# Keeping the first batch's y on the chip across a layer boundary, and making attention's first input in a written order

## The chip, the cores and the metric

The kernel runs on one core of a Trainium2 chip. The metric is device time in microseconds for one execution, lower is better. The core has five engines with queues of their own that run in order and wait for each other by semaphores: TensorE (PE, matmuls and transposes, with its weight loads shown apart as PEld), VectorE (DVE), ScalarE (ACT), GpSimd (POOL), and SyncE (SP), which here only issues DMAs. A view called the timeline lists the instructions with their start and length; "us from the span's start" is meant wherever a time of day is given.

## The reference

Input x has 8 batches of 2048 nodes with 256 features; adj is a 2048 by 2048 matrix. Everything is float32. Two layers follow each other:

```
# layer 0: graph convolution with batch norms, then residual and layer norm
A_norm = adj + eye
deg    = colsum(A_norm) + rowsum(A_norm) - diag(A_norm);  dinv = rsqrt(deg)
agg[b] = (A_norm * dinv[:, None] * dinv[None, :]) @ x[b]
h      = relu(batchnorm(agg @ W1.T + b1, g1, be1))      # 512 wide, statistics over all b and n
y      = batchnorm(h @ W2.T + b2, g2, be2)              # 256 wide, statistics over all b and n
x1     = layernorm(x + y)
# layer 1: attention with 4 heads of 64, masked where adj == 0, then residual and layer norm
q, k, v = x1 @ W
out    = layernorm(x1 + softmax(q k^T / 8 + mask) v)
```

The second batch norm needs the statistics of y over all batches before any y can be used. So layer 1 can't begin before layer 0 has ended for every batch.

## The kernel before

**Loading.** 16 row tiles of adj are loaded, turned by TensorE (L228) and copied into quarters T of 128 x 8 x 512 (`t0` to `t7`, 16 KB in a partition each). Row and column sums give dinv: `rsum` (L257, L260 on DVE), then a power on GpSimd (L97, in four pieces). `first_t1` (L208) is two DVE operations that compare and subtract in a quarter. The scheduler orders DVE here; SP and POOL go in the order of the text.

**Layer 0's products.** The aggregation is done with a scheme of seven products for every 2 by 2 block of halves (`product`, L320, eight steps of two matmul instructions), for units `(k, b, d)`: two halves of columns, pairs of batches, two halves of features. A unit needs forms of x: `scale` multiplies by dinv (on ACT for the first unit, L299; on GpSimd later, L293), and `s1` to `s4` (L304 to L318) add and subtract scaled forms on GpSimd. From the quarters, `t2`, `t3`, `t4` (L329 to L339) make differences on DVE. In the first unit the products come in the order p1, p2, p3 (which wants s4), p6 (s2 and t2), p7 (s3 and t3), p4 (t4), p5. `spread_dinv` sends dinv through DRAM into `dbc`, a row copied to all partitions, by which GpSimd scales the results `ag` (L402 and others). `linear` (L349) applies W1 and writes h to DRAM (`h_d`), 1 MB for each chunk of 512 nodes of one batch.

**Layer 0's second linear.** The 32 chunks go in 16 pairs. The first two pairs are made in place from the last unit (L568); the others are read back (`read_h`, L467, SP's queue, seven pairs deep, into slots of the quarters). For each pair ACT applies batch norm and relu (L497), GpSimd makes four forms (L516), PE does seven products (L521), DVE adds them up into `Y` (tiles `ag00` to `ag11`, used in turn by every second pair) and takes statistics (L535). Each Y is written to `y_d` in DRAM (L551, L561). The order of the pairs ends with batch 0: chunks 0 and 1 in the last but one, 2 and 3 in the last. Then `bn2.root` (an aggregate on DVE, L109, and a power on GpSimd) and `bn2.affine` (three small DVE operations, L114 to L116) give the scale `sc2` and shift `sh2`. In all of layer 0 every engine's order is that of the text.

**Attention's input.** `Layer1Input` makes, for a chunk c of a batch: `load_y` (L662) and `load_x` (L666) from DRAM; `bn` (ACT, L670, two instructions); `norm`, a half at a time (PE transposes, L681; a DVE add to x, L685; statistics, L635 and L637); `root` (four small GpSimd operations, L95 to L643); `apply` (ACT, L647, four instructions); `turn` (PE transposes, L703, and an ACT copy into `x1t`, L709); `project` for q (copied by ACT, L740), k (copied by DVE, L742) and v (PE L747, copied by ACT, L754). For batch 0 chunks 0 to 3 are made one after the other ahead of attention, in an order that the scheduler chooses:

```
for c in range(NCH):
    inp.load_y(0, c)
    inp.load_x(0, c)
...
    inp.root(0, c)
    for half in range(2):
        inp.apply(0, c, half)
    for half in range(2):
        inp.turn(0, c, half)
    for w in range(3 if c < NCH - 1 else 0):
        inp.project(0, 0, c, w)
```

`yt`, the place for y, has one buffer.

**Attention.** 64 units (batch, pair of heads, chunk of 512 queries) of 16 steps, one for each tile of 128 keys. A step g has `scores` (PE, L790), `mask_scores` (DVE, L802), `exps` (ACT, L808), `weigh` (PE, L820) and `add_up` (GpSimd, sums of probabilities, L829 and L831). Scores run three steps ahead (`LEAD`). PE, DVE, ACT and POOL follow the text's order here. Other work, the ends of units and the input of later batches, is put into the steps by `at_step(unit, step, ...)`; so are the last chunk's projections of batch 0's first pair of heads, at steps 0.1, 6.1 and 10.1 of unit 0.

The tiles live in pools on one stack: the pools of layer 0 are closed before those of attention open, and new tiles wait for what lay under them.

Of the kernel before, what the change touches and what calls it, by code (L numbers as in the profile page):

```python
# [26 lines left out]
def tile_gcn_then_masked_attention(  # L27
# [15 lines left out]
    nc = tc.nc  # L43
# [91 lines left out]
    with tc.tile_pool(name="bt", bufs=1) as bp, tc.tile_pool(name="x", bufs=1) as xp:  # L135

        def quarter(slot, pool=None):
            return (pool or bp).tile([P, HT, CH], F32, name=f"t{slot}")

        w1s = bp.tile([P, ND, H], F32, name="w1s")  # L140
        st1 = bp.tile([P, NH, NALL, 6], F32, name="st1")
        dinv = bp.tile([P, NT], F32, name="dinv")
        mdiag = bp.tile([P, NT, P], U8, name="mdiag")
        T = {}
        for s, ij in enumerate(HALVES):
            T[0, ij] = quarter(s)
        for s, ij in enumerate(HALVES[:3]):
            T[1, ij] = quarter(4 + s)


        free = [f"x{i}" for i in range(9)]

        class Form:
            def __init__(self):
                self.name = free.pop(0)
                self.t = xp.tile([P, HT, P], F32, name=self.name)

            def done(self):
                free.append(self.name)

        def load_form(b, j, d):
            f = Form()
            nc.sync.dma_start(
                f.t,
                x[b, j * HT * P : (j + 1) * HT * P, d * P : (d + 1) * P].rearrange(
                    "(t p) d -> p t d", p=P
                ),
            )
            return f

        def mask_out(k, ij, m8):
            i, j = ij
            c0 = (j * NK + k) * CH
            nc.sync.dma_start(mask_d[:, i * HT : (i + 1) * HT, c0 : c0 + CH], m8)

        def mask_of(k, ij):

            i, j = ij
            m8 = bp.tile([P, HT, CH], U8, name="m8")
            nc.vector.tensor_scalar(m8, T[k, ij], 0.0, None, op0=ALU.is_equal)  # L180
            if i == j:
                for q in range(TPC):
                    m = k * TPC + q
                    nc.vector.tensor_copy(
                        m8[:, m, q * P : (q + 1) * P], mdiag[:, i * HT + m, :]
                    )
            mask_out(k, ij, m8)

        units = [(k, b, d) for k in range(NK) for b in range(0, B, 2) for d in range(ND)]
        S = {}  # L190

        with tc.tile_pool(name="bt7", bufs=1) as bp7, tc.tile_pool(
            name="stage", bufs=2
        ) as sp, tc.tile_pool(name="stage1", bufs=1) as sp1, tc.tile_pool(
            name="pst", bufs=4, space=PSUM
        ) as pst, tc.tile_pool(name="psc", bufs=1, space=PSUM) as psc, tc.manual_schedule(
            engines={ENG.SP, ENG.Pool}
        ):
            T[1, HALVES[3]] = quarter(7, bp7)
            m8 = bp.tile([P, HT, CH], U8, name="m8")  # L200
            rsum = sp1.tile([P, NT], F32, name="rsum")
            diag = sp1.tile([P, NT], F32, name="diag")

            pc = psc.tile([P, CH], F32, name="pc")
            order = [j * HT + (NK - 1) * TPC + q for j in range(2) for q in range(TPC)]
            order += [j * HT + q for q in range(TPC) for j in range(2)]

            def first_t1(engine, here):  # L208
# [4 lines left out]
            for n, t in enumerate(order):  # L213
# [31 lines left out]
                if k == 0 and j == 1 and q < 2:  # L245
                    first_t1(nc.gpsimd, here)
# [874 lines left out]
```

## Time and profile before

| | |
|---|---|
| median of 3 runs | 3677.39 us (3677.05 to 3677.88) |
| profiled execution | 3676.57 us, of which the profile's span covers 3674.7 us |
| busy: PE | 3595.0 us (98%) |
| busy: POOL / DVE / ACT | 2777.7 (76%) / 1989.6 (54%) / 1642.2 us (45%) |
| granted TensorE clock, mean | 0.989 |

The profile is one execution by the hardware's own profiler. Busy time says how long an engine worked; its idle time is put down to what ended it. Where an engine waited for several others, the last to come is named. A granted clock of 1.00 is TensorE's full clock. The three-run median is 0.8 us above the profiled execution.

### The profile page before, as it was taken

What the parts mean: (1) busy time and instruction counts of PE and PEld (TensorE: products, weight loads), DVE (VectorE), ACT (ScalarE), POOL (GpSimd) and SP (SyncE); (2) the same over time, 40 slices, a digit from 0 to 9 for tenths busy, and PEclk for the clock granted to TensorE, in tenths of its full rate; (3) what the DMA queues carried; (4) which work ended last, traced back from release to release, by engine and by line L of the source; (5) the groups of instructions that cost most, each with busy time, mean ns of one, the idle gap of its engine ahead of it and who ended that gap; (6) DMA issues with size and microseconds to landing.
All of it is one profiled execution on the core that took longest, in us unless ns stands there. A gap on an engine that the chain in (4) does not pass through costs nothing.

```text
span 3674.7 us, 55830 instructions
## 1 busy us (share of the span) xinstructions
PE 3595.0 (98%) x23055; PEld 1490.0 (41%) x23055; DVE 1989.6 (54%) x2927; ACT 1642.2 (45%) x2034; POOL 2777.7 (76%) x1460
## 2 busy tenths in 40 slices
PE   7999999999999889999999999999999999999997
PEld 4444444444444333343433343433343344343332
DVE  6112131221146546766676676676676676667665
ACT  5001101110135345565565565565566566566555
POOL 5434263434247549999999999999999999999996
PEclk9999999999999889999999999999999999999999
DMA  9122232221246400010010010001001001000000
GB/s 330 54 86 77 83 126 92 75 91 35 75 181 254 175 18 1 18 41 13 13 36 24 13 36 24 7 30 36 7 24 36 7 24 35 13 13 30 7 1 25
DMA packets 133465, 207.92 MB, mean 57 GB/s; under 512 B 6976, under 2 KB 114000, under 8 KB 122704
## 3 DMA queue, kind: packets, MB, share of 16 engines
q1 hardware_dynamic: 132880, 199.00, 15.7%
q8 instruction: 183, 3.00, 0.3%
q0 software_dynamic: 144, 4.19, 0.3%
q10 hardware_dynamic: 176, 1.06, 0.1%
q14 instruction: 82, 0.67, 0.1%
HBM read 128.72 MB, written 75.51 MB: 56 GB/s over the span
## 4 chain that ended last, share of the span: by engine, by line
PE 95%; DVE 1%; POOL 1%; DMA 1%; ACT 1%; issue 0%; SPq 0%; DVEq 0%; POOLq 0%; ACTq 0%
PE out_ps L820 25%; PE st L790 24%; PE pa L323 21%; PE pm L735 6%; PE ph L356 5%; PE pa L521 5%; PE pm L747 3%; PE pm L847 2%; PE pm L681 1%; PE pm L703 1%; PE pm L874 1%; PE ps L228 1%; PE pm L861 1%; POOL acc L831 1%; PE ph L568 1%; DMA bt_d<-t 0%
## 5 line engine op out<-in xcount | busy, mean ns | idle before, releaser
L831 POOL TENSOR_TENSOR acc<-acc,prob 128x1024 f32<-128x1024 f32 x823 | 1947.8, 2367 | 103.0 <-ACT prob L808 45.2
L802 DVE SCALAR_TENSOR_TENSOR prob<-mask,st 128x1024 f32<-128x1024 uint8 x1024 | 1243.2, 1219 | 607.5 <-PE st L790 583.5
L808 ACT ACTIVATE prob<-prob 128x1024 f32<-128x1024 f32 x1024 | 1082.4, 1057 | 940.2 <-DVE prob L802 920.4
L820 PE MATMUL out_ps<-prob,v 64*64 64x512 f32 x8192 | 1077.4, 596 | 1.7 <-DVE ot L836 1.7
L790 PE MATMUL st<-qt,kt 64*64 64x512 f32 x8192 | 1066.9, 590 | 1.0 <-DVE prob L802 0.9
L323 PE MATMUL pa<-t,x 128*128 128x512 f32 x1792 | 774.6, 594 | 12.9 <-POOL x L318 9.1
L790 PEld LDWEIGHTS st<-qt,kt 64*64 64x64 f32 x8192 | 313.0, 133 | 568.3 <-issue 530.4
L323 PEld LDWEIGHTS pa<-t,x 128*128 128x128 f32 x1792 | 341.7, 191 | 443.7 <-issue 427.9
L820 PEld LDWEIGHTS out_ps<-prob,v 64*64 64x64 f32 x8192 | 285.6, 133 | 513.4 <-issue 414.3
L402 POOL TENSOR_TENSOR ag<-ag,dbc 128x512 f32<-128x512 f32 x16 | 20.2, 1264 | 459.9 <-DVE ag L401 457.3
L360 ACT ACTIVATE h<-ph,b1s 128x512 f32<-128x512 f32 x112 | 76.9, 687 | 404.4 <-PE ph L356 404.4
L735 PE MATMUL pm<-x1t,wq 128*128 128x512 f32 x512 | 250.8, 614 | 2.4 <-ACT x1t L709 2.4
L384 ACT COPY ag<-pa 128x512 f32<-128x512 f32 x16 | 9.4, 586 | 434.5 <-PE pa L323 434.5
L356 PE MATMUL ph<-ag,w1s 128*128 128x512 f32 x448 | 193.4, 592 | 0.0
L829 POOL TENSOR_TENSOR acc<-prob 128x1024 f32<-128x1024 f32 x64 | 151.0, 2360 | 17.5 <-ACT prob L808 15.9
L647 ACT ACTIVATE x<-x,ln_nm,ln_rs 128x256 f32<-128x256 f32 x256 | 137.5, 586 | 24.3 <-POOL ln_nm L643 24.3
L747 PEld LDWEIGHTS pm<-wq,x1t 128*128 128x128 f32 x1024 | 119.5, 192 | 28.2 <-issue 28.2
L361 DVE BATCH_NORM_STATS2 st<-h 128x6 f32<-128x512 f32 x112 | 76.9, 692 | 99.1 <-ACT h L360 99.1
L735 PEld LDWEIGHTS pm<-x1t,wq 128*128 128x128 f32 x512 | 89.8, 195 | 98.1 <-issue 87.2
L356 PEld LDWEIGHTS ph<-ag,w1s 128*128 128x128 f32 x448 | 85.1, 190 | 107.1 <-issue 106.9
L747 PE MATMUL pm<-wq,x1t 128*128 128x128 f32 x1024 | 128.1, 278 | 0.0
L381 DVE TENSOR_TENSOR ag<-pa,ag 128x512 f32<-128x512 f32 x16 | 11.1, 692 | 203.1 <-PE pa L323 203.1
(126 smaller groups left out, 2553.1 us busy)
## 6 DMA issues: line engine op xcount, KB each, us to landing
x<-in_x_dram SPq DMA_DIRECT2D x96, 512.0 KB, 4.2
h_d<-h SPq DMA_DIRECT2D x28, 1024.0 KB, 3.9
t<-h_d SPq DMA_DIRECT2D x28, 1024.0 KB, 7.0
a<-in_adj_dram SPq DMA_DIRECT2D x16, 1024.0 KB, 5.0
y_d<-ag SPq DMA_DIRECT2D x32, 512.0 KB, 2.9
yt<-y_d SPq DMA_DIRECT2D x32, 512.0 KB, 3.2
out_dram<-x SPq DMA_DIRECT2D x32, 512.0 KB, 2.9
bt_d<-t SPq DMA_DIRECT2D x4, 2048.0 KB, 16.2
```

The source lines that it names most:

```text
L323: nc.tensor.matmul(pa, s.t[:, m, :], t[:, m, :], start=(m == 0), stop=(m == HT - 1))
L356: nc.tensor.matmul(ph, w1s[:, d, f * P : (f + 1) * P], ag[:, d, :], start=(d == 0), stop=(d == ND - 1),)
L521: nc.tensor.matmul(py, w[:, f, :], t[:, f, :], start=(f == 0), stop=(f == 1))
L647: nc.scalar.activation(self.t[:, i, :], self.t[:, i, :], AF.Identity, bias=self.nm[:, i : i + 1], scale=self.rs[:, i : i + 1],)
L735: nc.tensor.matmul(pm, wq[:, d, wcols], xt[:, d, cols], start=(d == 0), stop=(d == ND - 1))
L747: nc.tensor.matmul(pm[:, j * P : (j + 1) * P], xt[:, d, t * P : (t + 1) * P], wq[:, d, wcols], start=(d == 0), stop=(d == ND - 1),)
L790: nc.tensor.matmul(st[r * HD : (r + 1) * HD, h, :], kt[hs, j * P + r * HD : j * P + (r + 1) * HD], qt[hs, cols], start=True, stop=True,)
L802: nc.vector.scalar_tensor_tensor(p, mask[:, j, cols][:, None, :].to_broadcast([P, 2, CH]), MASKED, st, op0=ALU.mult, op1=ALU.add,)
L808: nc.scalar.activation(probs[g], probs[g], AF.Exp)
L820: nc.tensor.matmul(outs[u][hs, r, :], inp.qkv[b, hp][2][rs, j, hs], probs[g][rs, h, :], start=(j == 0), stop=(j == NT - 1),)
L829: nc.gpsimd.tensor_add(accs[u], probs[g - 1], probs[g])
L831: nc.gpsimd.tensor_add(accs[u], accs[u], probs[g])
```

## The change

- The two chunks of Y of each of the last two pairs, batch 0's four chunks, stay in their tiles (`y0`); attention's first input reads them there. They are still written to DRAM.
- Batch 0's x in node order is read into the tiles `h1` and `dbc` (`x0`), by four DMAs on SP's queue ahead of w2 and of the reads of h.
- Pools lie on two stacks, left and right. Layer 0's quarters and forms are on the left and are followed there by the mask, W and attention's input (`attn_in`); the pool `l0` with Y, h and dbc is on the right and is followed there by attention's other tiles. The slots of the quarters that the pairs use are dealt in another order.
- Both `bn2.root` and both `bn2.affine` follow each other after the last pair. W (`wq`) is read on GpSimd's queue, ahead of the mask.
- Batch 0's input is made in the text's order: for all four chunks bn, transposes of y (into the PSUM tiles of the scores), add, statistics and root; then chunk 0's apply, turn, k, q and v; chunk 1's apply and turn; the first three scores, with chunk 1's k and chunk 2's apply behind the second. The rest is put into unit 0 by `at_step`, and chunk 2's and 3's q into units 1 and 2.
- At the start, DVE follows the text's order too, with the add into `rsum` ahead of `first_t1`; in the first unit of products s1 to s4 are on DVE, s3 between t2 and t3; `spread_dinv`'s copy is on ACT.

The diff, without lines that only changed their indentation:

```diff
-    with tc.tile_pool(name="bt", bufs=1) as bp, tc.tile_pool(name="x", bufs=1) as xp:
+    left, right = ExitStack(), ExitStack()
+    bp = left.enter_context(tc.tile_pool(name="bt", bufs=1, side="left"))
+    xp = left.enter_context(tc.tile_pool(name="x", bufs=1, side="left"))
-        with tc.tile_pool(name="bt7", bufs=1) as bp7, tc.tile_pool(
-            name="stage", bufs=2
-        ) as sp, tc.tile_pool(name="stage1", bufs=1) as sp1, tc.tile_pool(
+    with tc.tile_pool(name="bt7", bufs=1, side="right") as bp7, tc.tile_pool(
+        name="stage", bufs=2, side="right"
+    ) as sp, tc.tile_pool(name="stage1", bufs=1, side="right") as sp1, tc.tile_pool(
-            engines={ENG.SP, ENG.Pool}
+        engines={ENG.SP, ENG.Pool, ENG.DVE}
-        with tc.tile_pool(name="l0", bufs=1, reuse_waits="tile") as lp, tc.tile_pool(
+    lp = right.enter_context(
+        tc.tile_pool(name="l0", bufs=1, side="right", reuse_waits="tile")
+    )
+    with tc.tile_pool(
-                nc.vector.tensor_copy(dt, pd)
+            nc.scalar.copy(dt, pd)
-            def s1(v):
+        def s1(v, engine=nc.gpsimd):
-                nc.gpsimd.tensor_add(S[v, 1].t, S[v, 1, 0].t, S[v, 1, 1].t)
+            engine.tensor_add(S[v, 1].t, S[v, 1, 0].t, S[v, 1, 1].t)
...
-            def s4(v):
+        def s4(v, engine=nc.gpsimd):
...
-            for s in (s1, s2, s4, s3):
-                s(0)
+        for s in (s1, s2, s4):
+            s(0, nc.vector)
-                    for t, slot in ((t2, 4), (t3, 5), (t4, 6)):
-                        t(0, slot)
+                t2(0, 4)
+                s3(0, nc.vector)
+                t3(0, 5)
+                t4(0, 6)
-            places = {0: 0, 1: 5}
+        places = {0: 4, 1: 2}
+        x0 = []
+        for n, (name, size) in enumerate((("h1", [P, NH, CH]), ("dbc", [P, N]))):
+            t = lp.tile(size, F32, name=name)
+            t = t if n else t.rearrange("p a b -> p (a b)")
+            for i in range(2):
+                tx = t[:, i * N // 2 : (i + 1) * N // 2].rearrange("p (t d) -> p t d", d=D)
+                nc.sync.dma_start(
+                    tx, x[0, len(x0) * CH : (len(x0) + 1) * CH].rearrange("(t p) d -> p t d", p=P)
+                )
+                x0.append(tx)
-            for n, slot in enumerate((6, 1, 3, 4, 2)):
+        for n, slot in enumerate((0, 5, 6, 1, 3)):
-                if n == len(pairs) - 1:
-                    bn2.root(1)
-            bn2.root(0)
-            bn2.affine(1)
-            bn2.affine(0)
-    mpool = ctx.enter_context(tc.tile_pool(name="mask", bufs=1, reuse_waits="tile"))
+    y0 = [t for n in (len(pairs) - 2, len(pairs) - 1) for t in Y[n]]
+    left.close()
+    mpool = ctx.enter_context(tc.tile_pool(name="mask", bufs=1, side="left", reuse_waits="tile"))
-    nc.sync.dma_start(wq, wqkv.rearrange("(c p) f -> p c f", p=P))
+    with tc.manual_schedule(engines={ENG.DVE, ENG.Pool}):
+        nc.gpsimd.dma_start(wq, wqkv.rearrange("(c p) f -> p c f", p=P))
+        for o in (1, 0):
+            bn2.root(o)
+        for o in (1, 0):
+            bn2.affine(o)
-            self.st = pool.tile([P, n, 6], F32, name="ln_st")
...
+            self.st = pool.tile([P, n, 6], F32, name="ln_st", bufs=NCH)
...
+            self.y_pool = pool
-            y = self.yt[b, c] = self.pool.tile([P, NO, CH], F32, name="yt", bufs=1)
+            y = self.yt[b, c] = self.y_pool.tile([P, NO, CH], F32, name="yt", bufs=1)
-            y = self.yt[b, c]
-            tiles = range(IT * half, IT * (half + 1))
-            for i in tiles:
+            self.turn_y(b, c, half, pm)
+            self.add_y(b, c, half, pm, self.x1[b, c])
+        def turn_y(self, b, c, half, pm):
+            y = self.yt[b, c]
+            for i in range(IT):
+                r0 = (IT * half + i) * P
-                        pm[:, i % IT, o * P : (o + 1) * P], y[:, o, i * P : (i + 1) * P], ident
+                        pm[:, i, o * P : (o + 1) * P], y[:, o, r0 : r0 + P], ident
+        def add_y(self, b, c, half, pm, xt):
+            tiles = range(IT * half, IT * (half + 1))
+            here = slice(tiles[0], tiles[-1] + 1)
-            nc.vector.tensor_add(t[:, tiles[0] : tiles[-1] + 1], pm, t[:, tiles[0] : tiles[-1] + 1])
+            nc.vector.tensor_add(t[:, here], pm, xt[:, here])
-        def project(self, b, hp, c, which):
+        def project(self, b, hp, c, which, k_on_act=False):
+                elif k_on_act:
+                    nc.scalar.copy(dst, pm)
-            name="attn", bufs=2, reuse_waits="tile"
-        ) as ap_, tc.tile_pool(
-            name="ps_s", bufs=2, space=PSUM
-        ) as ps_s, tc.tile_pool(name="ps_o", bufs=1, space=PSUM) as ps_o, tc.tile_pool(
-            name="ps_m", bufs=2, space=PSUM
+            name="attn_in", bufs=2, side="left", reuse_waits="tile"
+        ) as ip, ExitStack() as late, tc.tile_pool(
+            name="ps_s", bufs=2, space=PSUM, reuse_waits="tile"
+        ) as ps_s, tc.tile_pool(
+            name="ps_o", bufs=1, space=PSUM, reuse_waits="tile"
+        ) as ps_o, tc.tile_pool(
+            name="ps_m", bufs=2, space=PSUM, reuse_waits="tile"
-            inp = Layer1Input(ap_, ps_m, NCH + 3)
+            inp = Layer1Input(ip, ps_m, NCH + 3)
+                if b:
+            for j, c in ((0.1, 2), (4.1, 3)):
+                for half in range(2):
+                    at_step(0, j, inp.turn, 0, c, half)
+            for half in range(2):
+                at_step(0, 1, inp.apply, 0, 3, half)
+            for j, c, w in (
+                (1.1, 1, 2), (2.1, 2, 1), (5.1, 2, 2), (6.1, 3, 1), (8.1, 1, 0), (10.1, 3, 2)
+            ):
+                at_step(0, j, inp.project, 0, 0, c, w)
+            for c in (2, 3):
+                at_step(c - 1, 3.1, inp.project, 0, 0, c, 0)
+            with tc.manual_schedule(engines=IN_ORDER):
-                inp.load_y(0, c)
-                inp.load_x(0, c)
+                    inp.yt[0, c] = y0[c]
+                    inp.x1[0, c] = ip.tile([P, TPC, D], F32, name="x1", bufs=NCH + 3)
+                    pm = ps_s.tile([P, TPC, D], F32, name="st")
-                    inp.norm(0, c, half)
+                        pmh = pm[:, half * IT : (half + 1) * IT, :]
+                        inp.turn_y(0, c, half, pmh)
+                        inp.add_y(0, c, half, pmh, x0[c])
+                right.close()
+                ap_ = inp.y_pool = late.enter_context(
+                    tc.tile_pool(name="attn", bufs=2, side="right", reuse_waits="tile")
+                )
+                def ready(c):
+                    if c < 2:
-                for w in range(3 if c < NCH - 1 else 0):
-                    inp.project(0, 0, c, w)
-            with tc.manual_schedule(engines=IN_ORDER):
+                ready(0)
+                inp.project(0, 0, 0, 1, k_on_act=True)
+                inp.project(0, 0, 0, 0)
+                inp.project(0, 0, 0, 2)
+                ready(1)
+                    if g == 1:
+                        inp.project(0, 0, 1, 1)
+                        ready(2)
```

The reads of y for batch 0 and its `load_x` are gone; for the other seven batches nothing is changed in what attention does, step by step.

## The prediction

> **What bounds the kernel now.** I read the page's first two parts, the list of who waited for whom on TensorE, the timeline, and a table of stretches, in that order. The page has TensorE busy for 3595.0 of 3674.7 us, so only about 80 us can come from filling it; a little more lies in matmuls that run at a lowered clock. The waits say where. Columns: who waited for what, us in total, times, longest.
>
> ```profile
> PE pm L703 <- ACT x L647: 16.5, 4, 5.0
> PE pm L681 <- ACT yt L670: 11.1, 1, 11.1
> PE pa L323 <- POOL x L318: 9.1, 1, 9.1
> PE pm L735 <- ACT x1t L709: 2.4, 3, 0.9
> ```
>
> Three of the four lie between the layers, the third at the start of layer 0. The stretches (length, busy us and count of PE, weight loads, DVE, ACT, POOL; then granted clock, DMA share, GB/s) show that the clock adds to this:
>
> ```profile
> 1271.70:1289.50 17.80, 11.85 (x40) 7.00 (x41) 3.69 (x11) 5.84 (x10) 1.68 (x4) 0.59 0.61 200
> 1303.00:1318.20 15.20, 9.09 (x44) 5.72 (x41) 4.96 (x12) 7.44 (x13) 8.71 (x7) 0.84 0.10 34
> 1318.20:1339.50 21.30, 15.39 (x44) 7.83 (x44) 3.74 (x11) 5.08 (x9) 1.66 (x4) 0.66 0.08 25
> 1410.00:3600.00 2190.00, 2188.78 (x18648) 863.19 (x18640) 1488.70 (x2196) 1297.58 (x1542) 2079.53 (x1068) 1.00 0.06 20
> ```
>
> The last line is attention at work: PE idle 1.2 us of 2190 at full clock, so whatever is won before it reaches the end. The first three are its entrance, idle and at a clock of 0.59 to 0.84.
>
> **Part 1, the start of layer 0.** The timeline there (start, length):
>
> ```profile
> 62.65 9.45 ACT L299 ACTIVATE x<-x,dinv 128x128 f32<-128x128 f32 x32 [4.07 <-POOL dinv L97]
> 69.84 5.74 POOL L306 TENSOR_TENSOR x<-x,x 128x1024 f32<-128x1024 f32 x1 [4.29 <-ACT x L299]
> 82.15 6.40 POOL L318 TENSOR_TENSOR x<-x,x 128x1024 f32<-128x1024 f32 x1
> 88.60 41.64 PE L323 MATMUL pa<-t,x 128*128 128x512 f32 x93 [9.13 <-POOL x L318]
> ```
>
> GpSimd makes s1, s2, s4 in turn, each in 5.7 to 6.4 us beside VectorE's big subtractions (2.34 when alone, from L306's median), and the third product waits until 88.60. The change gives s1 to s4 to DVE ahead of t2. DVE took 4.43 us for 128x4096 (L331), so 1.15 for 128x1024. The scales end at 69.7 for the third form and 72.1 for the fourth. s1 and s2 then end at 72.0, s4 at 73.2, t2 at 77.6, s3 at 78.8, t3 at 83.2, t4 at 87.6. The second product ends at 79.3 (72.44 and 16 times 0.43); so the third starts there, t2's product needs it at 86.2, t3's at 93.1, t4's at 100: all in time. The 9.1 us wait goes, with 0.2 about it, and with it the slow restart: after 88.60 four matmuls came 0.85 us apart instead of 0.43, 1.7 us. Further, the last add into rsum (L260 at 61.22) now stands before first_t1's 3.5 us on DVE, so dinv could come 1.9 us earlier; but GpSimd's power operations then run beside first_t1, and beside these two DVE operations L244 took 2.24 us instead of 0.46. I take 0.5, with -1.5 and 2 as ends. c11's add stands behind t4 on DVE as before (86.47 then, about 87 now), and GpSimd, freed of 21 us (L306, L310, L318, L314), has the next unit's scales ready earlier than before (95 against 100.2). What DVE's added 4.6 us could delay is covered by PE's two products, 13.7 us. Gain 11.5 us, from 9 to 13.
>
> **Part 2, between the layers.**
>
> ```profile
> 1258.70 1.88 PE L521 MATMUL pa<-t,h 128*128 128x512 f32 x4
> ...
> 1265.67 0.16 DVE L116 TENSOR_TENSOR sh<-be2s,rs 128x1 f32<-128x1 f32 x1
> 1270.86 1.52 ACT L670 ACTIVATE yt<-yt,sh,sc 128x512 f32<-128x512 f32 x2 [19.96 <-DMA yt<-y_d]
> 1271.73 2.25 PE L681 MATMUL pm<-ident,yt 128*128 128x128 f32 x8 [11.15 <-ACT yt L670]
> ...
> 1278.98 2.38 PE L703 MATMUL pm<-ident,x 128*128 128x128 f32 x8 [5.00 <-ACT x L647]
> ```
>
> Before: layer 0's last matmul ends at 1260.4 (1258.70 and 4 times 0.43), and the first weigh (L820) starts at 1339.51: 79.1 us. What PE does in it, at full clock: 64 transposes at 0.13 (four L874 hold it 0.53) 8.4; ten projections, seven of q and k at 1.72 and three of v at 1.79, 17.4; four score steps at 0.86, 3.4. That is 29.2, so 49.9 us are lost to waits and clock.
>
> After: both bn2 roots now follow the last stats on DVE, but one aggregate no longer stands ahead of the last y, and sh2 is ready at the same 1265.8. ACT starts bn at once, not at 1270.86: 5 us from the reload. From here the order of issue of the changed kernel, clock counted from 1265.9, fixes the rest. ACT runs eight bn at 0.72, until 5.8. DVE does add, two stats, two aggregates per half, 1.65 us by rows L685, L635, L637, so 3.3 per chunk from 2.5 on: 5.8, 9.1, 12.4, 15.7. PE turns y in 2.1 us per chunk at half clock; the fourth waits for the second chunk's add to free its PSUM tile (8.2) and ends at 10.3. GpSimd's root of chunk 0 takes 1.85 (5.8 to 7.7), ACT applies until 9.9, so PE goes straight on to turn chunk 0 (12.5); ACT's last copy ends at 13.3. K at half clock 3.4 (16.7), Q 1.9 (18.6), V 1.8 (20.4); ACT copies v (21.1), applies chunk 1, PE turns it 21.7 to 23.4: this is what is late next, 1.3 us of PE behind ACT. Then scores 0, scores 1, K of chunk 1, scores 2 and 3: 5.2. Chunk 2's apply stands on ACT between exps 1 and 2, and its turn on PE ahead of the first weigh: PE waits some 0.5 us and turns in 1.1. First weigh at 30.8, that is 1296.7.
>
> So 36.3 us in place of 79.1. Work moved behind the first weigh (Q1 to Q3, K2, V1, V2, one turn): 4 times 1.72, 2 times 1.79, 1.06, together 11.5, plus about 0.2 for each of seven breaks in the stream, 1.4. What hides the rest: unit 0 then has about 39 us of PE work, against 24 on ACT (16 exps of 1.06, and 7 of copies and applies) and 37 on GpSimd (15 sums of 2.44). Gain 79.1 - 36.3 - 12.9 = 29.9 us.
>
> The price not seen is the clock. Bursts of eight transposes ran at 0.50 at 1271.7, 1278.9, 1314.9 and 1332.7, but each followed a gap of about 5 us or more; in the first 59 us, where two thirds of PE's work is transposes, the clock was 1.00. I take half clock until Q. If transposes wake it, PE is 5 us earlier; if it stays at half through the first weigh, 8 later, and a further handoff of 2 us is possible. Gain 20 to 36. The Trainium skill's "TensorE: Matmul & The Clock Gate", part 4 on PE-mode transpose, says that transposes do not count as busy for this gate in the same way; by it alone the entrance would stay at half clock until K0, which makes the same 1296.7, while the row of the start would make about 1291.5.
>
> **Part 3, edits that should cost nothing.** The four x0 reads (2 MB) go on SP's queue ahead of w2 and the h reads; the two into dbc wait for its last multiplication (1040.0). Queued behind: w2 and ten h reads that started between 1010.5 and 1038.8. w2 arrives 5 us later (about 1047 against needed at 1040 by GpSimd), which holds W[1..4] and then the first bn1 root by 2 to 3 us; ACT wants that root only at 1052.28. h of pair 2 is wanted at about 1074; 3.5 MB at this stretch's 189 GB/s for a 0.48 share, some 390 when full, are there by 1052. Bound 0 to 2 us lost, taken 0. wq moves to GpSimd's queue, issued at 1251.8 behind the last form; only the mask's issue (0.79) is in the trace, and wq took 9.9 to land on SP; it is wanted at 1279. Batch 0's y is still written; the tail is untouched.
>
> **Sum.** 3676.57 - 11.5 - 29.9 = 3635.2 for the profiled execution, whose span is 3674.7; the median of the three runs is 0.8 above it: 3636. Bounds: gains of 29 to 49, so 3628 to 3648.
>
> **Rivals.** A: a new wait in place of the old. The chain root, apply, turn, project of one chunk is still serial; if PE never wakes and each of four handoffs costs 2 us more, the gain between the layers falls to about 15: 3651. For it: clocks of 0.59 to 0.84 above. Against: apply and stats of the next chunk now overlap. B: GpSimd is the bound. It is busy 2079.5 of 2190 us. Then only the start of its sums counts, 1303.5 before, about 1294 now, with 11.5 more: 3656. Against: PE's 1.2 us of idleness. C, slower: h arrives late because x0 stands ahead of it. A pair needs 3.15 MB in 12.0 us, and the thirteenth slice of the page moved 254 GB/s. To eat 41 us and 8 more, each of 14 pairs must come 3.5 us late, that is below about 203 GB/s: 3685. Against: 0.48 share. D: the change does not take effect, say because a tile of the new stack waits for an old one: 3677; the issue order shows bn reading the kept tiles and no y read for batch 0.
>
> **Numbers.** Forecast 0.76, A 0.10, B 0.06, C 0.05, D 0.03. A measurement of this kernel can tell about 0.2%, 7.4 us, from no change. Faster is forecast, A and B, 0.92; same 0.03; slower 0.05. The range takes in A and reaches a little below the lower bound: 3624 to 3652.
>
> **What would show it.** Right: PE's wait on s4 is gone, the third product starts at about 79; ACT's first bn at about 1254 (11.5 earlier than 1265.9); first weigh near 1285; in unit 0 no PE wait over 1 us. Wrong: a wait of PE on DVE's t2 or on GpSimd's scales before 125; a granted clock of 0.5 from bn to the first weigh; PE waiting for h or forms between 1050 and 1250; GpSimd ending after PE in the last unit.

## The result, and the profile after

The changed kernel takes 3641.39 us (median of 4 runs, 3639.95 to 3641.58) beside 3677.51 us for the kernel before in the same set (4 runs, 3677.05 to 3677.88). The ratio is 0.9901, with a 95% interval of 0.9884 to 0.9918: about 36 us faster, 5 us short of the 3636 forecast and inside its range. The profiled execution took 3641.23 us, with a span of 3639.4 us.

The waits of TensorE (who waited for what, us in total, times, longest) show that the four waits shown before are gone or smaller, and that a new one stands among them, the second line:

```profile
PE st L707 <- ACT ag L692: 6.1, 2, 5.9
PE st L707 <- DVE x L715: 5.3, 4, 1.5
PE pa L329 <- ACT x L305: 2.7, 1, 2.7
...
PE pm L733 <- ACT x L668: 1.5, 3, 1.2
...
PE pm L765 <- ACT x1t L739: 0.7, 1, 0.7
```

Lines have moved: L707 is now `turn_y`, L715 its add, L692 bn, L668 apply, L733 turn, L765 the q and k products, L824 scores, L854 weigh. The new wait is that of `turn_y` on VectorE's add.

**The start of layer 0**, in the timeline (start, length):

```profile
59.76 6.20 POOL L97 TENSOR_TENSOR dinv<-rsum,mhalf 128x4 f32<-128x4 f32 x4 [0.97 <-DVE rsum L263]
61.67 1.28 ACT L305 ACTIVATE x<-x,dinv 128x128 f32<-128x128 f32 x4 [2.99 <-POOL dinv L97]
71.87 63.68 PE L329 MATMUL pa<-t,x 128*128 128x512 f32 x148
83.38 0.59 ACT L390 COPY ag<-pa 128x512 f32<-128x512 f32 x1 [11.05 <-DMA bt_d<-t]
```

From 71.87 on TensorE runs 63.68 us without a break, where before it waited 9.1 us ahead of the third product, until 88.60. The powers on GpSimd take 6.20 us instead of 3.98 since they now run beside `first_t1`, but they begin earlier, and ACT's first scale starts at 61.67 instead of 62.65. The last line is a wait that the prediction did not see: ACT's first copy stands until 83.38, because its tile lies over a quarter that is still being written to DRAM. VectorE's queue hides it. Layer 0's last matmul ends at 1249.0 (1247.29 and four times 0.43) instead of 1260.4.

**Between the layers**, TensorE's part of the timeline:

```profile
1255.07 0.47 PE L707 MATMUL st<-ident,ag 128*128 128x128 f32 x1 [5.90 <-ACT ag L692]
...
1260.94 1.97 PE L707 MATMUL st<-ident,ag 128*128 128x128 f32 x8 [1.51 <-DVE x L715]
1264.42 1.97 PE L707 MATMUL st<-ident,ag 128*128 128x128 f32 x8 [1.51 <-DVE x L715]
1267.90 1.12 PE L707 MATMUL st<-ident,ag 128*128 128x128 f32 x4 [1.51 <-DVE x L715]
...
1271.40 5.89 PE L765 MATMUL pm<-x1t,wq 128*128 128x512 f32 x8 [0.68 <-ACT x1t L739]
1277.12 1.95 PE L779 MATMUL pm<-wq,x1t 128*128 128x128 f32 x16
...
1282.19 3.29 PE L824 MATMUL st<-qt,kt 64*64 64x512 f32 x16
...
1290.54 1.09 PE L854 MATMUL out_ps<-prob,v 64*64 64x512 f32 x8
```

Each burst of eight transposes is the second half of one chunk and the first half of the next, and before each of those shown stands 1.51 us of waiting for VectorE. Hence one chunk takes 3.48 us. The first weigh starts at 1290.54, 41.5 us after layer 0's end, where 36.3 were forecast and 79.1 stood before. The table of stretches (length; busy us and count of PE, weight loads, DVE, ACT, POOL; granted clock, DMA share, GB/s) gives the clock in it:

```profile
1249.00:1254.20 5.20, 0.17 (x1) 0.00 (x0) 4.40 (x11) 0.00 (x0) 1.58 (x4) 0.78 1.12 402
1254.20:1271.40 17.20, 10.11 (x41) 7.82 (x41) 12.94 (x40) 9.21 (x14) 5.62 (x14) 0.50 0.41 146
1271.40:1282.10 10.70, 9.20 (x32) 5.08 (x32) 0.00 (x0) 4.18 (x8) 1.22 (x3) 0.79 0.17 62
1282.10:1290.50 8.40, 8.40 (x46) 2.99 (x44) 4.84 (x5) 5.16 (x9) 2.37 (x1) 0.80 0.01 2
1290.50:1331.00 40.50, 40.22 (x313) 17.17 (x316) 19.11 (x17) 21.75 (x28) 30.67 (x13) 1.00 0.00 1
```

For 17.2 us TensorE is busy 59% of the time and runs at half clock. From the first weigh on it is busy 40.22 of 40.50 us at full clock, with the moved work inside the first unit: no new bound there.

### The profile page after: what moved, and what is told of

Read it like the earlier page. It is cut to its first block, busy times and chain, and to the rows that moved or that the text cites. A ratio compares the mean times of both kernels' runs of the same rounds, so it can differ in the third digit from the quotient of the medians.

```text
span 3639.4 us, 55807 instructions
## 1 busy us (share of the span) xinstructions
PE 3587.3 (99%) x23055; PEld 1487.6 (41%) x23055; DVE 1989.5 (55%) x2929; ACT 1642.6 (45%) x2036; POOL 2757.1 (76%) x1457
## 4 chain that ended last, share of the span: by engine, by line
PE 96%; POOL 1%; DVE 1%; ACT 1%; DMA 0%; issue 0%; SPq 0%; POOLq 0%; DVEq 0%; ACTq 0%
PE out_ps L854 25%; PE st L824 24%; PE pa L329 21%; PE pm L765 6%; PE ph L362 5%; PE pa L539 5%; PE pm L779 3%; PE pm L881 2%; PE pm L707 1%; PE pm L733 1%; PE ps L231 1%; PE pm L908 1%; PE pm L895 1%; POOL acc L865 1%; PE ph L584 1%; PE pc L241 0%
## 5 line engine op out<-in xcount | busy, mean ns | idle before, releaser
L865 POOL TENSOR_TENSOR acc<-acc,prob 128x1024 f32<-128x1024 f32 x823 | 1947.5, 2366 | 97.8 <-ACT prob L842 40.6
L854 PE MATMUL out_ps<-prob,v 64*64 64x512 f32 x8192 | 1077.1, 596 | 1.7 <-DVE ot L870 1.7
L824 PE MATMUL st<-qt,kt 64*64 64x512 f32 x8192 | 1064.2, 590 | 0.1
L824 PEld LDWEIGHTS st<-qt,kt 64*64 64x64 f32 x8192 | 312.8, 133 | 566.9 <-issue 528.3
L854 PEld LDWEIGHTS out_ps<-prob,v 64*64 64x64 f32 x8192 | 284.9, 132 | 511.6 <-issue 412.7
L765 PE MATMUL pm<-x1t,wq 128*128 128x512 f32 x512 | 247.2, 606 | 0.7 <-ACT x1t L739 0.7
L668 ACT ACTIVATE x<-x,ln_nm,ln_rs 128x256 f32<-128x256 f32 x256 | 137.4, 586 | 9.3 <-POOL ln_nm L664 9.3
L765 PEld LDWEIGHTS pm<-x1t,wq 128*128 128x128 f32 x512 | 88.2, 192 | 95.9 <-issue 89.1
L299 POOL TENSOR_TENSOR x<-x,dinv 128x1024 f32<-128x1024 f32 x60 | 116.7, 1966 | 0.0
```

The lines of the kernel that those rows point to most:

```text
L668: nc.scalar.activation(self.t[:, i, :], self.t[:, i, :], AF.Identity, bias=self.nm[:, i : i + 1], scale=self.rs[:, i : i + 1],)
L765: nc.tensor.matmul(pm, wq[:, d, wcols], xt[:, d, cols], start=(d == 0), stop=(d == ND - 1))
L824: nc.tensor.matmul(st[r * HD : (r + 1) * HD, h, :], kt[hs, j * P + r * HD : j * P + (r + 1) * HD], qt[hs, cols], start=True, stop=True,)
L854: nc.tensor.matmul(outs[u][hs, r, :], inp.qkv[b, hp][2][rs, j, hs], probs[g][rs, h, :], start=(j == 0), stop=(j == NT - 1),)
L865: nc.gpsimd.tensor_add(accs[u], accs[u], probs[g])
```

## The experiments

Three sets of four kernels ran, each set on one chip together with the kernel before (medians 3678.53, 3678.19 and 3677.32 us, 9 runs each). Each ratio has an interval of about 0.0015 to either side, so the differences of a few us below are held by traces too, not by the times alone. The last column is the time from layer 0's last matmul to the first weigh in the profiled run (ends counted as above).

| kernel | median us | to before, us | ratio (95% interval) | entrance, us |
|---|---|---|---|---|
| the change | 3641.39 | -36.1 | 0.9901 (0.9884 to 0.9918) | 41.5 |
| e1 both halves of turn_y first | 3636.63 | -41.9 | 0.9884 (0.9869 to 0.9899) | 37.5 |
| e2 start undone | 3654.10 | -24.4 | 0.9933 (0.9920 to 0.9947) | 41.4 |
| e3 only s1 to s4 back on GpSimd | 3652.65 | -25.9 | 0.9926 (0.9913 to 0.9940) | 40.6 |
| e4 y read back from DRAM | 3642.78 | -35.8 | 0.9903 (0.9888 to 0.9918) | 43.4 |
| e5 all input ahead of the scores | 3649.93 | -27.4 | 0.9926 (0.9912 to 0.9939) | 68.7 |
| e6 11 matmuls in the gap | 3641.47 | -36.7 | 0.9901 (0.9886 to 0.9916) | 40.1 |
| e6t 44 transposes in the gap | 3640.26 | -37.9 | 0.9897 (0.9882 to 0.9913) | 40.6 |
| e6b matmuls between all halves | 3648.63 | -29.6 | 0.9921 (0.9908 to 0.9935) | 48.4 |
| e7 e1 and long fillers | 3638.62 | -39.6 | 0.9894 (0.9879 to 0.9909) | 38.1 |
| e8 e1 and short fillers | 3633.34 | -44.0 | 0.9880 (0.9865 to 0.9895) | 34.0 |
| e9 e8 and the first score earlier | 3632.19 | -45.1 | 0.9878 (0.9863 to 0.9893) | 31.5 |
| e10 x0 read last | 3639.38 | -37.9 | 0.9898 (0.9883 to 0.9913) | 38.1 |

The change, e2, e3 and e10 have the same entrance in their text, and their traces show 41.5, 41.4, 40.6 and 38.1 us for it. So a difference of up to 3.4 us between the entrances of two single traces does not yet speak for an edit; e10 below shows where it can come from.

### e1: is the new wait the missing 5 us?

```diff
-                        inp.turn_y(0, c, half, pmh)
-                        inp.add_y(0, c, half, pmh, x0[c])
+                        inp.turn_y(0, c, half, pm[:, half * IT : (half + 1) * IT, :])
+                    for half in range(2):
+                        inp.add_y(0, c, half, pm[:, half * IT : (half + 1) * IT, :], x0[c])
```

> Both halves of a chunk's turn_y stand ahead of its two adds, all else as in the changed kernel (3641.4 us). Theory 1, the miss of some 5 us between the layers is a new wait: the second half's transposes write the PSUM tile that the first half's add reads, so TensorE and VectorE took turns, 3.48 us a chunk. Then the fourth chunk's turn_y ends near 1265 instead of 1269, the first weigh starts some 4 us earlier, and the time is 3637 (3635.5 to 3638.5). Theory 2, VectorE's chain (3.3 us a chunk by its rows) or the apply of chunk 0 set this stretch, not the wait: then TensorE only idles elsewhere, and the time stays at 3641 (within 1.5).

Measured 3636.63 us (3634.38 to 3636.99), theory 1. Its runs do not overlap with those of the change. TensorE's timeline:

```profile
1255.59 3.46 PE L707 MATMUL st<-ident,ag 128*128 128x128 f32 x15 [0.23 <-ACT ag L692]
1259.80 1.94 PE L707 MATMUL st<-ident,ag 128*128 128x128 f32 x8 [0.75 <-DVE x L715]
1262.96 1.94 PE L707 MATMUL st<-ident,ag 128*128 128x128 f32 x8 [1.22 <-DVE x L715]
1264.69 1.91 PE L733 MATMUL pm<-ident,x 128*128 128x128 f32 x8
1267.28 5.56 PE L765 MATMUL pm<-x1t,wq 128*128 128x512 f32 x8 [0.68 <-ACT x1t L739]
```

The four waits, 5.3 us together, have become two of 0.75 and 1.22, ahead of the third and fourth chunk, which are for the two PSUM tiles to come free. The prediction had such a wait ahead of the fourth chunk alone. K starts at 1267.28; the forecast had put it at 1267.5. So the wait of a half chunk on the add of the other half, in the same PSUM tile, was the larger part of the miss. Text order alone removed it.

### e2 and e3: what the start is worth, and which edit earns it

e2 takes the start back as a whole (s1 to s4 on GpSimd, dinv spread behind t4 through VectorE, VectorE not held to text order); e3 only the sums:

```diff
-        for s in (s1, s2, s4):
-            s(0, nc.vector)
+        for s in (s1, s2, s4, s3):
+            s(0)
...
-                s3(0, nc.vector)
```

> The changed kernel with the start of layer 0 as before: s1 to s4 on GpSimd ahead of the first unit, dinv spread behind t4 through VectorE, and VectorE not held to text order in the adjacency stage. If the start is worth what the trace after shows (layer 0 ends 11.4 us earlier) and adds to the rest, this takes 3652.8 (3651.3 to 3654.3), and TensorE waits about 9 us for s4 again. Rival: the gain at the start is partly given back later, since attention's GpSimd is busy 95% of the time: then less than 9 us are lost, under 3650.5.

> The changed kernel with only the four sums s1 to s4 of the first unit back on GpSimd; VectorE keeps its text order, and dinv's spread stays ahead of t2. If the move of the sums to VectorE carries the start's gain, nearly all is lost: dinv is still some 1 us earlier than before, so 10 to 11 us, 3651 to 3653. Rival: the earlier dinv and the order on VectorE carry a good part of it: then 3 us or more of the 11.4 remain, under 3650.

e2 lies 24.4 us under the kernel before where the whole change lies 36.1 under it: the start is worth 11.7, and no part of it is seen to be given back in attention. e3 lies 25.9 under it: the sums on VectorE carry 10.2 of these 11.7, and without them the earlier dinv is good for about 1.5, a figure inside the scatter of the two kernels. In e3's timeline the sums are slow again beside VectorE's subtractions, and TensorE waits for the third, although ACT's first scale starts at 62.04, earlier than the 62.65 before:

```profile
82.78 6.40 POOL L324 TENSOR_TENSOR x<-x,x 128x1024 f32<-128x1024 f32 x1
89.24 17.04 PE L329 MATMUL pa<-t,x 128*128 128x512 f32 x32 [9.87 <-POOL x L324]
```

### e4: is it y on the chip that pays?

```diff
                     inp.yt[0, c] = y0[c]
+                    nc.sync.dma_start(y0[c], y_d[c])
```

> The changed kernel, but each of batch 0's four y tiles is read back from DRAM into its own place ahead of bn, so that y makes the round trip again; everything else, the order of text included, stays. The prediction put 5 us on the reload. Theory 1: bn of the first chunk starts 5 us later, near 1259.5, and the time is 3646.5 (3645 to 3648). Theory 2: chunks 0 and 1 were written 12 us before layer 0's end and are back in time, only the last two wait, and TensorE turns those behind others anyway: then under 2.5 us are lost, 3641 to 3644, and the 5 us before were the wait of the reload for memory that layer 0 still held.

Measured 3642.78 us, 1.4 above the change's median and 0.4 by the distances to before: theory 2. ACT's first bn in e4 starts at the same time as in the change (1254.27 and 1254.20), although y comes from DRAM. The second, third and fourth chunk wait for their reads, 1.29, 3.86 and 3.47 us:

```profile
1254.27 1.52 ACT L692 ACTIVATE ag<-ag,sh,sc 128x512 f32<-128x512 f32 x2 [14.71 <-DVE sh L116]
1257.07 1.52 ACT L692 ACTIVATE ag<-ag,sh,sc 128x512 f32<-128x512 f32 x2 [1.29 <-DMA ag<-y_d]
1262.45 1.52 ACT L692 ACTIVATE ag<-ag,sh,sc 128x512 f32<-128x512 f32 x2 [3.86 <-DMA ag<-y_d]
1267.43 1.52 ACT L692 ACTIVATE ag<-ag,sh,sc 128x512 f32<-128x512 f32 x2 [3.47 <-DMA ag<-y_d]
```

The prediction was right that bn starts 5 us earlier and wrong about why. SyncE's queue in the kernel before shows the place: the first read of y stands behind the write of the last y, though its own chunk was written at 1245.95.

```profile
1262.53 0.32 SPq L561 DMA_DIRECT2D y_d<-ag  x1
1263.03 1.91 SPq L662 DMA_DIRECT2D yt<-y_d  x1
```

That read then took 7.7 us to land. In e4 the reads of the first two chunks are issued at 1237.26 and 1242.33, before layer 0 ends, and the first is back in time. So the edit that the title names first, y kept on the chip, is worth 0.4 us here by the distances and 1.9 us of entrance in the traces; the rest of the gain between the layers comes without it. In the kernel before, the read was late both by its issue and by its length; whether it was the order of the queue or the place of `yt` in memory that held the issue was not separated.

### e5: is the input inside the first unit worth something?

The tasks at steps of unit 0 to 2 are dropped; behind chunk 0's projections stands instead

```diff
-                ready(1)
+                for c in range(1, NCH):
+                    ready(c)
+                    for w in (1, 2, 0):
+                        inp.project(0, 0, c, w)
```

(with the turns of chunks 2 and 3 in `ready`).

> The changed kernel, but all of batch 0's input (turns of four chunks, K, V and Q) is made ahead of the first scores and none inside the first unit; y is still kept on chip. Theory 1, TensorE bounds throughout: 12 us of its work only change places, nothing is lost but what the clock and the handoffs cost, 3642 (3640 to 3644). Theory 2, GpSimd's sums of exps are the bound of a unit without that work (15 of 2.44 us against some 28 us of TensorE): the first unit then lasts as long as with it, and 9 us or more are lost, less what GpSimd makes up later: 3646 to 3652.

Measured 3649.93 us, 8.7 above the change by the distances to before. The number is theory 2's, its mechanism is not. The first unit without the moved work, in a table of stretches:

```profile
1320.00:1340.00 20.00, 20.00 (x192) 7.19 (x188) 14.48 (x12) 12.06 (x12) 19.37 (x9) 1.00 0.00 1
```

GpSimd is busy 19.37 of 20 us there, but TensorE does not wait once. The loss is all in the entrance, 27.2 us longer (68.7 instead of 41.5), against 19.0 us less behind the first weigh (from 1317.87 to the span's end at 3647.7 are 2329.8 us, from 1290.54 to 3639.4 in the change 2348.9). In the 83 us from layer 0's end to 1332.0, TensorE is idle 5.3 us more than in the change (busy 63.47 of 82.63 us instead of 68.93 of 82.83), and the clock is 0.77 instead of 0.84. The waits name the idle time:

```profile
PE pm L733 <- ACT x L668: 4.5, 9, 1.2
PE pm L765 <- ACT x1t L739: 2.7, 4, 0.7
```

against 1.5 and 0.7 us in the change. So theory 1 had the right engine and had priced the handoffs too low: each chunk's chain of apply, turn, copy and projection stops TensorE, and inside the unit scores and weighs fill such places.

### e6, e6t, e6b: what the clock goes by

TensorE gets work that nobody reads, in the empty 5.9 us ahead of `turn_y` (e6; in e6t transposes, in e6b three more matmuls after each half but the last):

```diff
+                def warm(n):
+                    pm = ps_m.tile([P, CH], F32, name="pm")
+                    for i in range(n):
+                        nc.tensor.matmul(pm, ident, x0[3][:, 0:2, :], start=True, stop=True)
+
+                warm(11)
```

> The changed kernel with 11 matmuls of 128x512 added that TensorE runs in its empty 5.9 us between layer 0's last matmul and the first turn_y; their sums go to a PSUM tile that nothing reads. TensorE then comes to turn_y without a gap. Theory 1, the clock of 0.50 from bn to the first scores is the price of the gap alone: turn_y starts at full clock, K and Q of chunk 0 too, and the time falls by 4 to 5 us, to 3636.5 (3635.5 to 3638). Theory 2, transposes themselves do not hold the clock up (the rule that the prediction cites): only the first few microseconds of turn_y are fast, the clock is at half again by K at about 1271, and less than 2 us are won: 3639.5 to 3641.5.

> As the kernel with matmuls in the gap, but with 44 transposes of 128x128 in their place, the same columns through TensorE (4.9 us at full clock). Theory 1, any work holds the clock: the granted clock in the gap is as high as with matmuls and turn_y starts at full clock. Theory 2, transposes do not count: the clock falls to half inside the gap, the 44 take up to 9 us, overrun the gap by some 3 us, and turn_y and K run at half clock as before: 3643 to 3646.

> As the kernel with 11 matmuls in the gap, with three more of them after each half chunk of turn_y but the last, where TensorE waits 1.5 us for VectorE's add. If matmuls hold the clock where transposes do not, the clock stays above 0.9 through K, Q and V of chunk 0 and to the first weigh, and the time falls by 4 to 6 us, to 3636.5 (3635 to 3638). Rival: the entrance is bound by VectorE's adds and statistics and by ACT's apply, and a fast TensorE only waits longer for them: under 2 us won, 3639.5 or more.

Measured 3641.47, 3640.26 and 3648.63 us: no gain, no gain (e6t's 1.8 by the distances lies within the scatter), a loss of 6.5. As measures of a price e6 and e6b are inconclusive, for a float32 matmul of 128x512 shows as two instructions of 0.43 us and not one:

```profile
1250.07 9.61 PE L994 MATMUL pm<-dbc,ident 128*128 128x512 f32 x22
```

They ran 9.6 us instead of 4.7, overran the gap and pushed `turn_y` from 6.1 to 9.4 us behind layer 0's end; in e6b every place was overfilled as well, and with a clock of 1.00 through the whole entrance it lasted 48.4 us. In e6 the clock fell again inside `turn_y`, at 1263.67, behind 3.41 us with 1.09 us of work: the gap alone was not what cost it. What the traces do show is how the clock behaves. Read in steps of 0.1 us, it changes in the changed kernel at 1252.0, 1275.8, 1282.7 and 1286.1: these are apart by 7, 2 and 1 times 3.41 us, so within a run it is set on a fixed grid of 3.4 us, and in other runs the grid lies elsewhere. Between the points of that grid, in e6t, the stretches are:

```profile
1247.83:1251.24 3.41, 3.41 (x34) 3.41 (x32) 3.29 (x7) 0.00 (x0) 1.02 (x3) 1.00 0.95 354
1251.24:1254.65 3.41, 1.84 (x13) 1.18 (x11) 0.57 (x5) 2.22 (x4) 0.57 (x1) 1.00 0.79 244
1254.65:1258.05 3.40, 1.97 (x8) 1.57 (x8) 3.13 (x10) 3.04 (x6) 0.00 (x0) 0.50 1.05 394
```

The first is full of transposes and of nothing else, and the clock stays at 1.00 behind it. It falls after the second, in which TensorE was busy for 1.84 of 3.41 us. Theory 1 of e6t holds, its theory 2 fell: the 44 transposes took 4.97 us. (That the clock follows the window just ended, and not an older one, is seen in the change: layer 0 ends at 1249.0, and the clock falls at 1252.0.) The Trainium skill's "TensorE: Matmul & The Clock Gate", part 4 on PE-mode transpose, which the prediction weighed, says that transposes do not count as busy in the same way; here, for float32 transposes of 128x128, the measurement decides against it. The same page's part 1, on what is happening, describes a free-running window of about 3.4 us, and that agrees with the 3.41 us found here.

### e7, e8, e9: wait and clock taken together

e8 is e1 with fillers that end before the wait does, e7 the same with 11, 3, 4 and 2 in their places:

```diff
+                warm(6)
...
                     inp.root(0, c)
+                    if c:
+                        warm((1, 2, 1)[c - 1])
```

> Both halves of turn_y ahead of the adds (worth 4.8 us alone, 3636.6) together with matmuls in the places where TensorE still idles: 11 in the gap, then 3, 4 and 2 behind the second to fourth chunk. If wait and clock are separate prices they add: K and Q of chunk 0 take 3.5 us instead of 5.6 and the scores 1.7 instead of 3.6, and the time is 3632.5 (3631 to 3634). Rival: VectorE's chain of 12.6 us from the first add on is what is left, and the clock behind it is all there is to win, under 2 us: 3635 to 3636.6.

> Turn_y ahead of the adds with matmuls in TensorE's idle places, now sized so that they end before the wait does: a matmul of 128x512 showed as two instructions of 0.43 us, so 6 in the gap of 5.9 us, then 1, 2 and 1 (11, 3, 4 and 2 ended turn_y's wait 3.5 us late). If the clock has a price of its own beside the wait, turn_y, K, Q and the scores of chunk 0 run at full clock and the time is 3632.5 (3631 to 3634.5) against 3636.6 without the matmuls. Rival: VectorE's chain alone sets the pace: 3635.5 or more.

e7 took 3638.62 us, slower than e1: it has the overlong matmuls, and its `turn_y` starts at 1258.40, 9.4 us after layer 0's end. Its clock was 1.00 through the entrance: here a full clock bought with a later start is no gain. e8 took 3633.34 us, as expected if the clock has a price beside the wait; against e1 that is 2.1 us by the distances to before and 3.5 us of entrance in the traces. Its K and Q take 3.70 us instead of 5.56:

```profile
1264.48 1.04 PE L733 MATMUL pm<-ident,x 128*128 128x128 f32 x8
1266.25 3.70 PE L765 MATMUL pm<-x1t,wq 128*128 128x512 f32 x8 [0.73 <-ACT x1t L739]
```

but the clock still fell at 1275.0, behind a window of 3.41 us in which TensorE was busy for 1.91 us and had waited 1.2 us for chunk 1's apply. e9 puts the first score step there:

```diff
-                ready(1)
                 for g in range(LEAD):
                     mask_scores(g, scores(g))
+                    if g == 0:
+                        ready(1)
```

> As the kernel with the shorter matmuls, and the first score step stands ahead of chunk 1's apply and turn, where TensorE waited 1.2 us for ACT and the share of busy time fell below what kept the clock up. Expected 1 us less than that kernel, 3631.5 (3630 to 3633.5); if the first weigh is bound by the exponentials on ACT instead, no change from it.

Measured 3632.19 us, 1.1 under e8, as expected, though within the scatter of both. Its trace has the clock at 1.00 all through the entrance, which is 31.5 us. The wait of 1.2 us stands in e7 and e10 too, and there the clock did not fall behind it, so whether e9's order kept the clock or the place of its grid was not separated. By the same token part of e8's 2.1 us can be the grid: e10's K and Q took 3.70 us without any filler. e9 is faster than both kernels: 45 us under the kernel before (ratio 0.9878, 0.9863 to 0.9893), and 9 under the change.

### e10: the reads of x ahead of w2

> The changed kernel with the four reads of x for batch 0 behind the reads of h on SP's queue instead of ahead of w2. The prediction took the place of these reads as free, with up to 2 us lost. Theory 1, free: 3641.4 (3640 to 3643). Theory 2, the 7 us that GpSimd waits for h and w2 there reach TensorE: 1.5 to 2 us faster, 3639.5.

```diff
+        for c, tx in enumerate(x0):
+            nc.sync.dma_start(
+                tx, x[0, c * CH : (c + 1) * CH].rearrange("(t p) d -> p t d", p=P)
+            )
```

(behind `read_h`, and taken out above.) The median, 3639.38 us, is what theory 2 expects (1.8 us by the distances, within the scatter), but the trace shows that its mechanism is not at work. GpSimd's work on w2 does start 7 us earlier (1028.54 instead of 1035.58), and TensorE's second linear starts when it did, at 1053.81 instead of 1053.80; layer 0 ends at the same 1249.0. The profiled run is shorter in the entrance only, 38.1 us against 41.5, with the same instructions starting at the same times up to K:

```profile
1268.82 1.91 PE L734 MATMUL pm<-ident,x 128*128 128x128 f32 x8
1271.41 3.70 PE L766 MATMUL pm<-x1t,wq 128*128 128x512 f32 x8 [0.68 <-ACT x1t L740]
```

K and Q take 3.70 us here and 5.89 in the change, and the first two score steps 1.95 us and 3.29. The stretches between points of the grid, first two of e10 and then three of the change, tell why:

```profile
1267.85:1271.25 3.40, 2.82 (x12) 2.42 (x12) 2.64 (x10) 1.06 (x2) 1.62 (x5) 0.50 0.32 90
1271.25:1274.65 3.40, 3.24 (x8) 1.56 (x9) 0.00 (x0) 0.69 (x2) 1.38 (x3) 1.00 0.63 218
```

```profile
1269.00:1272.40 3.40, 2.73 (x10) 1.82 (x9) 1.66 (x5) 1.17 (x2) 1.62 (x5) 0.50 0.61 211
1272.40:1275.80 3.40, 3.40 (x5) 1.35 (x4) 0.00 (x0) 0.59 (x1) 0.28 (x2) 0.50 0.28 97
1279.25:1282.65 3.40, 2.08 (x12) 1.11 (x16) 0.00 (x0) 3.23 (x7) 0.00 (x0) 1.00 0.02 5
```

In e10 the grid fell so that 2.82 us of transposes lay in one window, and the clock rose after it. In the change the window around the same burst held 2.73 us, and the clock waited for the next; there it fell again at 1282.7, in e10 it did not. The 3.4 us are where the grid lay in that run. That the whole of the difference between the two medians is this was not shown; it would take many more runs of each.

## Why the prediction was right or wrong

**Part 1, right.** Forecast 11.5, measured 11.4 at layer 0's end and 11.7 in e2. The third product follows without a break, as the sum had it, and e3 confirms the cause, VectorE for GpSimd in s1 to s4. The 0.5 taken for dinv was 0.98 at the scale, inside its ends, and 0.57 at the second product (71.87 instead of 72.44). One side remark of the sum was wrong: the next unit's scales were to be ready at 95, earlier than before (100.2), and were ready at 102.3 (begun at 96.66, 5.60 us). GpSimd began late because dinv's row was late (its read was issued at 88.48 and took 6.7 us), behind the copy of ACT that waited until 83.38 for a write to DRAM. The prediction had not looked at what lies under that tile; VectorE's and TensorE's queues hid it.

**Part 2, right in most of its mechanism, one term too small.** Forecast 29.9, measured 79.1 - 41.5 - 13.7 = 23.9 (13.7 is what the stretch from first weigh to the end grew: 2348.9 us instead of 2335.2).

- bn at 1254.2, forecast 1254.4. The cause named for it, the round trip of y, fell in e4: the first reload can be hidden when it is issued early. In the kernel before it was issued at 1263.03 and took 7.7 us.
- The step that failed is "PE turns y in 2.1 us per chunk". This was TensorE's busy time. The pace is 3.48 us, as each half waits for the add of the half before it; the fourth chunk ends at 1269.0 and not at 1264.5. The prediction did look at PSUM tiles, but only at how many there are, not at the two halves inside one. e1 removes this and brings K to the forecast time; counted from layer 0's end K starts 3.9 us earlier there, of the 5.2 by which the entrance was longer than forecast.
- The clock was taken as half until Q, 3.4 and 1.9 us for K and Q; they took 5.89 together. Then it fell a second time, at 1282.7, which cost the scores 3.29 us for two steps instead of 1.72. That second fall was not in the sum. Of the two prices weighed, the row of the start and the page's rule, the time came out nearer the rule's, but for another reason: the transposes did count, and TensorE was too thinly busy with them, 59% of 17.2 us.
- Moved work cost 13.7 where 12.9 were forecast: near enough, and e5 shows that made ahead of the scores it would have cost 8.7 us more.
- Of the 23.9 us, e5 tests the work that moved and e4 the kept y. What the written order, the two stacks and x already in place each bring was not tested apart; for them stand only the waits that shrank in the trace (on ACT's apply from 16.5 to 1.5 us).

**Part 3, right.** The reads of x ahead of w2 held GpSimd's sums of w2 for 7.0 us and the first bn1 root by 2.6 us (1038.56 instead of 1035.97 in e10), where 2 to 3 were forecast for that root, and TensorE for none. wq and the mask landed in time.

**Sum.** 11.4 and 23.9 are 35.3; 3676.57 less that is 3641.3, beside 3641.23 measured. The parts are cut from the same two traces, so that they add up is no proof of them; the experiments are.

**The rivals.** A's two halves, a clock that stays low and a new wait between engines, both came in part, and the time lies between the forecast's 3636 and A's 3651. The wait was not one of A's four handoffs, though. B fell: in e5 GpSimd was at 97% of a stretch and TensorE waited for nothing. C fell with e10: the second linear starts at 1053.8 with or without the reads ahead of it. D fell with the trace, in which the waits are gone.

## What to carry to other kernels

When a step is split into halves so that two engines can overlap, see whether the halves share a tile: if so, write both halves before the first is read, or (not tried here) give each a tile of its own; otherwise the engines take turns. Cost a chain between engines by its pace, the work and the waits of one round, and not by the busy time of one of its engines. Before removing a round trip through memory, see whether it is late because of its length or because of its place in a queue; and let fillers for a gap on TensorE end before the wait does: those that overran it cost time (e6b), those that did not came with some 2 us (e8), part of which can be the grid of the clock.

## What the runs showed of the hardware

- The granted clock changes only at points 3.41 us apart, and it goes with how busy TensorE was in the window before. It rose after windows with 2.82 us or more of 3.41 (e10, e6) and not after 2.73 (the change) or 2.80 (e6, 62.17 to 65.59). For its fall busy time gives no such line: it fell after 2.08 (the change), 1.91 (e8) and 1.84 (e6t), and it stayed after 2.25 (e10, 1274.65 to 1278.05), but also after 1.96 (e8, 1254.57 to 1257.98) and after the two windows below, the first of the change, the second of the kernel before. What else decides is open; the ends of matmuls are modelled in the profile, so busy time in short bursts is not exact.

```profile
1060.80:1064.21 3.41, 2.06 (x6) 0.73 (x5) 1.44 (x2) 3.41 (x6) 2.64 (x2) 1.00 0.00 0
77.92:81.33 3.41, 1.55 (x4) 0.38 (x2) 3.41 (x2) 0.00 (x0) 3.41 (x1) 1.00 1.05 452
```

- Transposes of 128x128 in float32 can hold the clock up (e6t, a window of 3.41 us full of them) and raise it (e10, a window with 2.82 us of them). What kept it at half for 17 us was a wait of 1.51 us before every 1.97 us of work, not that the work was transposes.
- The place of that grid differs from run to run, and with it the entrance: 3.4 us between e10 and the change, whose instructions began at the same times up to K.
- Four powers on GpSimd took 6.20 us beside VectorE's two operations of `first_t1`, and 3.98 where these had ended before them.
